# Attention and FP4 feed-forward on one core: loading the first batch's rows once, and ordering the first loads

## The chip, the cores and the metric

The kernel runs on one core of a Trainium2 chip. The metric is the device time of one execution in microseconds (us). Three runs of the kernel before gave 3693.88, 3696.45 and 3697.93; the median is 3696.45. One further execution was profiled.

The core's engines work side by side, each through its own list of instructions in order: TensorE (PE in the profile; its weight loads are PEld), VectorE (DVE), ScalarE (ACT), GpSimd (POOL) and SyncE (SP). SP here only issues transfers. Transfers of all engines share 16 DMA engines.

## The reference

The input x has 4 batches of 2048 rows of 256 numbers. One transformer block is computed:

```python
q, k, v = heads(x @ Wq.T), heads(x @ Wk.T), heads(x @ Wv.T)        # 16 heads of 16
attn = softmax(q @ k.T / 4)                                         # 2048 x 2048 for each head
x1 = layernorm(x + merge(attn @ v) @ Wo.T)
xq = fp4(x1)                                                        # blocks of 16 along a row
h = silu(xq @ fp4(w_gate).T) * (xq @ fp4(w_up).T)                   # 704 wide
out = layernorm(x1 + fp4(h) @ fp4(w_down).T)
```

All is float32; `fp4` rounds to a 4-bit grid with one scale for each block of 16 and scales back.

## The kernel before, in words

**Tiling.** A step is one batch, one block of 512 query rows (four in a batch, `NQB`) and one group of four heads: 64 steps. A step goes through 16 periods, one for each 128 keys. In a period PE computes a tile of scores for the row maxima (`maxima`, written `pm`; DVE takes the maximum, `mx`), the scores once more with the maximum subtracted (`exponentials`, `pe`; ACT takes the exponential, `e`), and the product with the values (`values`, `av`). The maxima run `LEAD` = 20 periods ahead of the exponentials. So the main loop starts with 20 lead periods, 0 to 19, in which there are only maxima and other work, and the first exponentials come in lead period 20. The program is written out in this order: PE keeps it, the other engines' lists are ordered by a scheduler.

**Other work in the periods.** Into each period goes a part (two in a lead period) of the work in `queue`: projections of x, the preparation of the weights, the feed-forward of a block whose attention is finished. `project` (L300) takes a block of 512 rows of x in `xb`, turns it on PE (`ptx`, two parts), has ACT copy it out (`xT`), and multiplies by the transposed weights (`pq` for keys and queries, `pv` for values). Which products a call makes is in `what`: `k0` and `q0` are keys and queries of heads 0 to 7, `k1` and `q1` of heads 8 to 15, `v` the values. A call makes only some of them, so the same rows are loaded and turned several times: in the first batch a block is projected for `k0`, for `v`, for `k1` and for the queries.

**Keys and queries go through device memory.** A product is split into a high and a low part (`hi`, three buffers, cast by ACT; `lo`, two buffers, by POOL from a copy of the product, `read`, two buffers). SP stores both into `kx` or `qx` (L329, four stores each). From there `load_q` (L354) and `load_k` (L363) fetch what a step needs, again on SP: four loads of 62 rows of 2 KB for the queries, four loads of 64 rows of 2 KB for each block of 512 keys. Values are stored to `vx` (L346, from two tiles `vt`) and loaded by `load_v`. Each transfer issued by SP is one instruction in SP's order; transfers take turns on eight semaphores, and one that takes a semaphore again waits until the transfer before it on the same semaphore has landed.

**Buffers for x.** `xb` (L197) has two buffers. `feed_forward` loads the same rows once more into `x1` (L588, two buffers of the same size in another pool), as the residual.

**The start.** The first two blocks of x are loaded by SP, the three weights by ACT (L207), behind which ACT fills the constant rows of `kx` (L212, four transfers of 128 KB). PE turns Wk, Wq and Wv (L214). Then lines 681 to 692 project the keys of the first batch's four blocks, and the queries of the first, with loads of x, q and k set between them. The values of the four blocks, then `k1` and `q1`, are put into `queue` and are worked off in the lead periods; the remaining queries come after them, interleaved with the preparation of the feed-forward's weights (`prepare`).

The row maxima need the keys of four periods at a time: lead periods 0, 4, 8 and 12 of the first step each begin a new block of 512 keys. In lead periods 8 to 14 the loads for the second step are asked for.

Of the kernel before, what the change touches and what calls it, by code (L numbers as in the profile page):

```python
# [31 lines left out]
F32 = mybir.dt.float32  # L32
# [6 lines left out]
P = 128  # L39
# [10 lines left out]
QT = QB // P  # L50
# [23 lines left out]
def block_kernel(  # L74
# [13 lines left out]
    B, L, D = x.shape  # L88
    FF = w_gate.shape[0]
    KC = D // P  # L90
    NQB = L // QB
# [14 lines left out]
    def psum(name):  # L106
        banks["n"] += 1
        if banks["more"] and banks["n"] % 2:
            return ps_m.tile([P, 2, 512], F32, tag="pm", name=name)[:, 0, :]
        return ps_x.tile([P, 512], F32, tag="px", name=name)  # L110
# [22 lines left out]
    def matmul(*args, **kw):  # L133
        tc.keep_in_program_order(nc.tensor.matmul(*args, **kw))  # L134

    def transpose(*args):
        tc.keep_in_program_order(nc.tensor.transpose(*args))  # L137

    def read(bank):

        t = p2.tile([P, QB // 2], F32, tag="read", name="read")[:, : bank.shape[1]]
        nc.scalar.copy(t, bank)  # L142
        return t
# [31 lines left out]
    wqT = const.tile([P, KC, D], F32, tag="wqT", name="wqT")  # L175
    wkT = const.tile([P, KC, D], F32, tag="wkT", name="wkT")
    wvT = const.tile([P, KC, D], F32, tag="wvT", name="wvT")
# [13 lines left out]
    p1 = ctx.enter_context(tc.tile_pool(name="p1", bufs=1))  # L191
    p2 = ctx.enter_context(tc.tile_pool(name="p2", bufs=2))
    xb_of = {}

    def load_x(b, tb):
        rows = slice(tb * QB, (tb + 1) * QB)
        xb_of[b, tb] = p2.tile([P, QT, D], F32, tag="xb", name="xb")  # L197
        nc.sync.dma_start(xb_of[b, tb], x[b, rows, :].rearrange("(t p) d -> p t d", p=P))

    load_x(0, 0)  # L200
    load_x(0, 1)


    loaded = {}
    for name, w in (("wk", wk), ("wq", wq), ("wv", wv)):
        loaded[name] = p2.tile([P, KC, D], F32, tag="xnh", name=name, bufs=3)
        nc.scalar.dma_start(loaded[name], w.rearrange("(c p) k -> p c k", p=P))  # L207
    ones = p2.tile([P, 2 * NC * L // P], F32, tag="a", name="ones")
    nc.gpsimd.memset(ones, 1.0)
    for i in range(2):  # L210
        for c in range(KC):
            nc.scalar.dma_start(kx[i][c][RM:R].rearrange("r h (a n) -> (r h a) n", n=2 * NC * L // P), ones)  # L212

    for name, dst in (("wk", wkT), ("wq", wqT), ("wv", wvT)):  # L214
        for kc in range(KC):
            pt = psum("ptw")
            for n in range(KC):
                transpose(pt[:, n * P : (n + 1) * P], loaded[name][:, n, kc * P : (kc + 1) * P], ident)
            if name == "wv":
                nc.vector.tensor_copy(dst[:, kc, :], pt[:, :D])  # L220
                continue

            for n in range(KC):
                nc.vector.tensor_copy(
                    dst[:, kc, n * P : (n + 1) * P].rearrange("p (d h) -> p d h", h=NC),
                    pt[:, n * P : (n + 1) * P].rearrange("p (h d) -> p d h", h=NC),
                )


    RF = FF // 8  # L230
# [69 lines left out]
    def project(b, tb, what):  # L300

        rows = slice(tb * QB, (tb + 1) * QB)
        if (b, tb) not in xb_of:
            load_x(b, tb)
        xb = xb_of.pop((b, tb))
        xT = p2.tile([P, KC, QB], F32, tag="xT", name="xT", bufs=1)
        yield 0
        for kc in range(KC):
            pt = psum("ptx")
            for t in range(QT):  # L310
                transpose(pt[:, t * P : (t + 1) * P], xb[:, t, kc * P : (kc + 1) * P], ident)
            nc.scalar.copy(xT[:, kc, :], pt)
            yield 600
        for name, c in [(w[0], int(w[1])) for w in what if w != "v"]:
            w, dst = (wkT, kx[b % 2][c][:, :, rows]) if name == "k" else (wqT, qx[(b * NQB + tb) % len(qx)][c])
            hi = p2.tile([P, QB], F32R, tag="hi", name=name + "hi", bufs=3)
            lo = p2.tile([P, QB], F32R, tag="lo", name=name + "lo", bufs=2)
            for half in range(2):
                cols = slice(half * QB // 2, (half + 1) * QB // 2)
                pq = psum("pq")[:, : QB // 2]  # L320
                for kc in range(KC):
                    matmul(pq, w[:, kc, c * P : (c + 1) * P], xT[:, kc, cols], start=(kc == 0), stop=(kc == KC - 1))
                nc.scalar.copy(hi[:, cols], pq)
                nc.gpsimd.tensor_tensor(lo[:, cols], read(pq), hi[:, cols].bitcast(F32), ALU.subtract)
                yield 900

            for i, half in enumerate((hi, lo, hi, lo) if name == "k" else (hi, hi, lo, lo)):
                d = min(DH, RM - i * DH)
                nc.sync.dma_start(  # L329
                    dst[i * DH : i * DH + d].rearrange("r h n -> (r h) n"), half[: d * NC, :].bitcast(F32)  # L330
                )
            projected.add((b, tb, name + str(c)))
        for t in range(QT if "v" in what else 0):
            v = vt[t // 2]
            pv = psum("pv")
            for kc in range(KC):
                matmul(
                    pv[:, :D], xT[:, kc, t * P : (t + 1) * P], wvT[:, kc, :], start=(kc == 0), stop=(kc == KC - 1)
                )
            src = pv[:, :D].rearrange("p (g i j d) -> p g i j d", g=NG, i=NP, j=2)  # L340
            for j in range(2):
                nc.scalar.copy(v[:, :, t % 2, :, 2 * j * DH : (2 * j + 1) * DH], src[:, :, :, j, :])
            if t % 2:
                t0 = tb * QT + t - 1
                for g in range(NG):
                    nc.sync.dma_start(vx[b % 2][g, :, t0 : t0 + 2, :], v[:, g].rearrange("p t i c -> p t (i c)"))  # L346
            if t == QT - 1:
                projected.add((b, tb, "v"))
            yield 900
# [4 lines left out]
    def load_q(s):  # L354
        b, qb, g = steps[s]
        for i in range(NP):
            c, h = divmod(g * HG + i * 2, NC)
            q = p1.tile([P, QB], F32R, tag="q", name="q", bufs=3 * NP)
            for j in range(2):
                nc.sync.dma_start(  # L360
                    q[R * j : R * j + RM, :].bitcast(F32), qx[(b * NQB + qb) % len(qx)][c][:RM, h + j, :]
                )
            q_sb[s, i] = q  # L363

    def load_k(s, kb):
        b, qb, g = steps[s]
        for i in range(NP):
            c, h = divmod(g * HG + i * 2, NC)
            k = p1.tile([P, QB], F32R, tag="k", name="k", bufs=20)
            for j in range(2):  # L370
                nc.sync.dma_start(
                    k[R * j : R * j + R, :].bitcast(F32), kx[b % 2][c][:, h + j, kb * QB : (kb + 1) * QB]
                )
            k_sb[s, i, kb] = k
# [291 lines left out]
    def projection(b, tb, what=("k0", "q0", "v", "k1", "q1")):  # L666
        return project(b, tb, what)
# [13 lines left out]
    for tb in range(NQB):  # L681
        for _ in projection(0, tb, ("k0", "q0") if tb == 0 else ("k0",)):
            pass
        if tb + 2 < NQB:
            load_x(0, tb + 2)
        if tb == 1:
            load_q(0)
        if tb > 0:
            load_k(0, tb - 1)
    load_k(0, NQB - 1)  # L690
    load_x(0, 0)
    load_x(0, 1)
    for tb in range(NQB):
        queue.append(projection(0, tb, ("v",)))
    for tb in range(NQB):
# [4 lines left out]
    for n in range(-LEAD, N + LAG):  # L700
# [10 lines left out]
        if n > 0 and kt % QT == 0:  # L711
            ahead, kb = divmod(n - QT + 2 * NKT, NKT)
            if ahead < len(steps):
                b, qb, g = steps[ahead]
# [60 lines left out]
```

## Time and profile before

| | |
|---|---|
| median of three runs | 3696.45 us |
| the profiled execution's own time | 3695.37 us |
| its span, first to last instruction | 3693.6 us |
| PE busy | 3540.7 us, 96% of the span |
| DVE busy | 2805.0 us, 76% |
| ACT busy | 2694.0 us, 73% |
| POOL busy | 1293.4 us, 35% |
| loads of x into `xb` | 27, of 512 KB each |
| loads of x into `x1` | 16, of 512 KB each |
| bytes moved by DMA | 334.18 MB, mean 90 GB/s |

How to read it: a row such as `PE L137 MATMUL ptx<-ident,xb` names the engine, the line, the operation and what is written from what. Most PE products are recorded by helper lines: L134 is every product, L137 every transpose, so they are told apart by the tiles. `SPq` is SP's issuing of a transfer, not the transfer itself. The granted PE clock is given as a share of full speed. Idle time of an engine counts only where that engine holds up the end.

### The profile page before, as it was taken

What the parts mean: (1) busy time and instruction counts of PE and PEld (TensorE: products, weight loads), DVE (VectorE), ACT (ScalarE), POOL (GpSimd) and SP (SyncE); (2) the same over time, 40 slices, a digit from 0 to 9 for tenths busy, and PEclk for the clock granted to TensorE, in tenths of its full rate; (3) what the DMA queues carried; (4) which work ended last, traced back from release to release, by engine and by line L of the source; (5) the groups of instructions that cost most, each with busy time, mean ns of one, the idle gap of its engine ahead of it and who ended that gap; (6) DMA issues with size and microseconds to landing.
All of it is one profiled execution on the core that took longest, in us unless ns stands there. A gap on an engine that the chain in (4) does not pass through costs nothing.

```text
span 3693.6 us, 57860 instructions
## 1 busy us (share of the span) xinstructions
PE 3540.7 (96%) x21396; PEld 1602.0 (43%) x21396; DVE 2805.0 (76%) x3250; ACT 2694.0 (73%) x5452; POOL 1293.4 (35%) x1542
## 2 busy tenths in 40 slices
PE   5889999999999999999999999999999999999995
PEld 4433444444444444444444444444443434444343
DVE  3777777787787877878787787778778788878834
ACT  2667777777777777777777777777777777777772
POOL 0331432424243242423424243342424325241425
PEclk8899999999999999999999999999999999999997
DMA  6643333223232332323323232322322221222100
GB/s 217 188 137 117 93 91 105 81 85 115 68 114 84 94 94 85 109 70 109 95 78 106 85 97 88 97 89 74 113 75 63 75 79 57 75 68 86 47 7 6
DMA packets 197954, 334.18 MB, mean 90 GB/s; under 512 B 26024, under 2 KB 75560, under 8 KB 197672
## 3 DMA queue, kind: packets, MB, share of 16 engines
q1 hardware_dynamic: 196280, 329.16, 29.2%
q8 instruction: 171, 2.80, 0.3%
q10 hardware_dynamic: 1392, 1.31, 0.1%
q14 instruction: 111, 0.91, 0.1%
HBM read 242.81 MB, written 86.51 MB: 89 GB/s over the span
## 4 chain that ended last, share of the span: by engine, by line
PE 82%; DVE 11%; DMA 2%; POOL 2%; SPq 1%; issue 1%; ACT 1%; ACTq 0%; POOLq 0%; DVEq 0%
PE av L134 24%; PE pe L134 18%; PE pm L134 16%; DVE mx L397 8%; PE pz L134 5%; PE pg L134 5%; PE pu L134 5%; PE pq L134 3%; PE pth L137 1%; PE pv L134 1%; PE pa L137 1%; PE py L134 1%; PE pn L137 1%; DMA k<-kx 1%; DMA xb<-in_L_attn_x_dram 1%; DVE amax L149 1%
## 5 line engine op out<-in xcount | busy, mean ns | idle before, releaser
L397 DVE TENSOR_REDUCE mx<-pm 128x2 f32<-128x1024 f32 x2048 | 2407.9, 1217 | 706.8 <-PE pm L134 702.5
L431 ACT ACTIVATE e<-pe 128x512 f32<-128x512 f32 x4096 | 2217.9, 595 | 671.2 <-PE pe L134 666.0
L134 PE MATMUL av<-e,v 128*32 128x512 f32 x8192 | 1098.3, 608 | 0.0
L134 PE MATMUL pe<-q,k 64*128 64x512 f32 x4096 | 1037.2, 456 | 4.8 <-ACT e L431 4.4
L134 PEld LDWEIGHTS pe<-q,k 64*128 64x128 f32 x4096 | 476.4, 185 | 969.0 <-ACT e L431 855.7
L134 PE MATMUL pm<-k,q 62*128 62x512 f32 x4096 | 803.8, 448 | 60.0 <-DVE mx L397 53.0
L134 PEld LDWEIGHTS pm<-k,q 62*128 62x128 f32 x4096 | 347.0, 186 | 373.2 <-issue 178.6
L134 PEld LDWEIGHTS av<-e,v 128*32 128x32 f32 x8192 | 162.2, 108 | 332.2 <-issue 314.1
L537 POOL TENSOR_TENSOR a<-a,g 128x352 f32<-128x352 f32 x124 | 116.4, 939 | 499.5 <-ACT a L536 499.5
L582 POOL TENSOR_TENSOR x<-x,read 128x128 f32<-128x128 f32 x128 | 58.9, 460 | 493.6 <-ACT read L142 493.6
L134 PE MATMUL pz<-wdT,hT 128*128 128x128 f32 (+1 forms) x1536 | 230.0, 292 | 0.0
L163 POOL TENSOR_TENSOR xn<-xn,m 128x704 f32<-128x704 f32 (+2 forms) x104 | 159.5, 1534 | 157.7 <-DVE m L162 139.0
L134 PEld LDWEIGHTS pz<-wdT,hT 128*128 128x128 f32 (+1 forms) x1536 | 191.0, 191 | 45.5 <-ACT e L431 18.2
L551 POOL TENSOR_TENSOR h<-a,u 128x352 f32<-128x352 f32 x124 | 116.2, 937 | 226.7 <-ACT u L550 224.4
L134 PE MATMUL pg<-wgT,xqT 128*128 128x352 f32 x512 | 187.4, 489 | 0.0
L513 POOL TENSOR_TENSOR x<-x,read 128x256 f32<-128x256 f32 x64 | 46.7, 730 | 400.2 <-ACT read L142 399.9
L134 PE MATMUL pu<-wuT,xqT 128*128 128x352 f32 x512 | 186.1, 486 | 0.0
L164 POOL TENSOR_TENSOR xn<-xn,m 128x704 f32<-128x704 f32 (+2 forms) x104 | 159.8, 1536 | 5.6
L165 POOL TENSOR_TENSOR xn<-xn,sc 128x704 f32<-128x704 f32 (+2 forms) x104 | 131.5, 1264 | 7.8
L538 POOL TENSOR_TENSOR a<-a,g 128x352 f32<-128x352 f32 x124 | 118.8, 958 | 9.7
L134 PEld LDWEIGHTS pg<-wgT,xqT 128*128 128x128 f32 x512 | 88.3, 191 | 58.5 <-ACT e L431 19.1
L134 PEld LDWEIGHTS pu<-wuT,xqT 128*128 128x128 f32 x512 | 88.2, 191 | 58.7 <-ACT e L431 20.0
(95 smaller groups left out, 2283.1 us busy)
## 6 DMA issues: line engine op xcount, KB each, us to landing
k<-kx SPq DMA_DIRECT2D x1024, 128.0 KB
v<-vx SPq DMA_DIRECT2D x64, 768.0 KB
q<-qx SPq DMA_DIRECT2D x256, 124.0 KB
kx<-khi SPq DMA_DIRECT2D x64, 256.0 KB
qx<-qhi SPq DMA_DIRECT2D x64, 256.0 KB
xb<-in_L_attn_x_dram SPq DMA_DIRECT2D x27, 512.0 KB
vx<-vt SPq DMA_DIRECT2D x128, 96.0 KB
x<-in_L_attn_x_dram SPq DMA_DIRECT2D x16, 512.0 KB
```

The source lines that it names most:

```text
L134: tc.keep_in_program_order(nc.tensor.matmul(*args, **kw))
L137: tc.keep_in_program_order(nc.tensor.transpose(*args))
L163: engine.tensor_tensor(xn, xn, m, ALU.add)
L164: engine.tensor_tensor(xn, xn, m, ALU.subtract)
L165: engine.tensor_tensor(xn, xn, sc.unsqueeze(2).to_broadcast([p, nb, FB]), ALU.mult)
L397: nc.vector.tensor_reduce(mx_sb[s][:, t, 2 * i : 2 * i + 2, kb], pm, AX.X, ALU.max)
L431: nc.scalar.activation(e, pe[j], AF.Exp, scale=SCALE)
L513: nc.gpsimd.tensor_add(x1[:, t, :], x1[:, t, :], read(py[:, :D]))
L537: engine.tensor_mul(a, a, g)
L538: engine.tensor_add(a, a, g)
L551: engine.tensor_mul(h[:, cols], a, u)
L582: nc.gpsimd.tensor_add(x1[:, t, cols], x1[:, t, cols], read(pz))
```

## The change

The first batch's four blocks of x are loaded once, at the start, and stay in their buffers for all their products: blocks 0 and 1 in the two `xb` buffers, blocks 2 and 3 in the two `x1` buffers, which the feed-forward doesn't need yet. `xb_of` is no longer emptied by `project`, so a later projection of the same block finds it there. The transposes of x are still made for every projection. In the first stage each block's k loads are put right behind its stores, and for block 0 the q loads right behind those; before, a block's k loads came one block later, and q after block 1. Wv is asked for last on ACT's queue among the weights, ahead of the constant fills in both built programs, and it is turned by PE after the keys of all four blocks instead of ahead of the first. In the built program the first transfers of SP are the four blocks of x and Wo, where before they were two blocks of x, Wo and two blocks for `x1`.

```diff
     def load_x(b, tb):
         rows = slice(tb * QB, (tb + 1) * QB)
-        xb_of[b, tb] = p2.tile([P, QT, D], F32, tag="xb", name="xb")
+        if b == 0 and tb >= 2:
+            xb_of[b, tb] = p1.tile([P, QT, D], F32, tag="x1", name="xb", bufs=2)
+        else:
+            xb_of[b, tb] = p2.tile([P, QT, D], F32, tag="xb", name="xb")
         nc.sync.dma_start(xb_of[b, tb], x[b, rows, :].rearrange("(t p) d -> p t d", p=P))
-    load_x(0, 0)
-    load_x(0, 1)
     loaded = {}
-    for name, w in (("wk", wk), ("wq", wq), ("wv", wv)):
+    def load_w(name, w):
         loaded[name] = p2.tile([P, KC, D], F32, tag="xnh", name=name, bufs=3)
         nc.scalar.dma_start(loaded[name], w.rearrange("(c p) k -> p c k", p=P))
+    load_x(0, 0)
+    load_w("wk", wk)
+    load_w("wq", wq)
+    for tb in range(1, NQB):
+        load_x(0, tb)
     ones = p2.tile([P, 2 * NC * L // P], F32, tag="a", name="ones")
...
-    for name, dst in (("wk", wkT), ("wq", wqT), ("wv", wvT)):
+    load_w("wv", wv)
+    def turn_w(name, dst):
         for kc in range(KC):
             pt = psum("ptw")
...
+    turn_w("wk", wkT)
+    turn_w("wq", wqT)
...
-        xb = xb_of.pop((b, tb))
+        xb = xb_of[b, tb]
...
     for tb in range(NQB):
         for _ in projection(0, tb, ("k0", "q0") if tb == 0 else ("k0",)):
             pass
-        if tb + 2 < NQB:
-            load_x(0, tb + 2)
-        if tb == 1:
+        load_k(0, tb)
+        if tb == 0:
             load_q(0)
-        if tb > 0:
-            load_k(0, tb - 1)
-    load_k(0, NQB - 1)
-    load_x(0, 0)
-    load_x(0, 1)
+    turn_w("wv", wvT)
     for tb in range(NQB):
         queue.append(projection(0, tb, ("v",)))
```

## The prediction

> **What bounds the kernel now.** I read the page's 40 slices first, then busy time by stretch, PE's waits in the first 400 us, and PE's and SP's timelines of the first 60.
>
> Busy time by stretch (columns: us, length, then busy PE, PEld, DVE, ACT, POOL with counts; granted PE clock; DMA share; GB/s):
> ```profile
> 38.00:57.40 19.40, 3.41 (x12) 2.56 (x12) 2.36 (x2) 0.59 (x1) 0.00 (x0) 0.50 0.71 225
> 57.40:62.00 4.60, 4.60 (x13) 3.02 (x12) 2.36 (x2) 1.02 (x3) 0.00 (x0) 0.50 0.50 145
> 149.00:200.00 51.00, 50.29 (x312) 21.65 (x312) 42.60 (x56) 41.48 (x87) 23.68 (x26) 1.00 0.52 166
> 315.00:3600.00 3285.00, 3241.99 (x19869) 1441.26 (x19868) 2573.23 (x2959) 2507.22 (x5032) 1160.68 (x1380) 1.00 0.28 85
> ```
> From 315 to 3600 PE is busy 98.7% of the time: there it is the bound, and the change leaves that stage's instructions alone. What it can win lies before 315. From 38 to 57.4 PE does 3.4 us of work, and is then still at half clock. What PE waits for up to 400 us (total, times, longest):
> ```profile
> PE ptx L137 <- DMA xb<-in_L_attn_x_dram: 31.4, 6, 13.8
> PE pm L134 <- DVE mx L397: 17.2, 15, 7.1
> PE pm L134 <- DMA k<-kx: 5.3, 1, 5.3
> ```
> PE's timeline (start, length; idle time before it in brackets):
> ```profile
> 29.27 1.94 PE L137 MATMUL ptx<-ident,xb 128*128 128x128 f32 x8 [5.85 <-DMA xb<-in_L_attn_x_dram]
> 40.18 1.55 PE L134 MATMUL pm<-k,q 62*128 62x512 f32 x4 [5.33 <-DMA k<-kx]
> 55.54 1.94 PE L137 MATMUL ptx<-ident,xb 128*128 128x128 f32 x8 [13.81 <-DMA xb<-in_L_attn_x_dram]
> 57.41 1.22 PE L134 MATMUL pm<-k,q 62*128 62x512 f32 x4
> 65.56 1.10 PE L137 MATMUL ptx<-ident,xb 128*128 128x128 f32 x8
> 140.18 1.09 PE L137 MATMUL ptx<-ident,xb 128*128 128x128 f32 x4 [6.01 <-DMA xb<-in_L_attn_x_dram]
> ```
> The rows for 40.18 and 57.41 are the score maxima of lead periods 0 and 1; the x reload at 55.54 stands between them. SP's queue says why:
> ```profile
> 24.61 2.36 SPq L360 DMA_DIRECT2D q<-qx  x4
> 27.02 4.77 SPq L371 DMA_DIRECT2D k<-kx  x4
> 31.89 0.54 SPq L329 DMA_DIRECT2D kx<-khi  x1
> 34.61 0.35 SPq L329 DMA_DIRECT2D kx<-klo  x1
> 37.09 0.32 SPq L329 DMA_DIRECT2D kx<-khi  x1
> 39.62 0.32 SPq L329 DMA_DIRECT2D kx<-klo  x1
> 51.21 1.08 SPq L198 DMA_DIRECT2D xb<-in_L_attn_x_dram  x2
> ```
> The x reload goes out at 51.21 because everything above stands before it. The stores at 34.61, 37.09 and 39.62 each waited for one of the q loads (SP's waits put 6.4 us on three such waits): the four q loads land about 2.5 us apart, and the k loads issued behind them only at 40.06.
>
> **What the skill says.** "DMA: Bandwidth & Descriptors", section "Why a DMA increments its semaphore by 16 and not by 1": a transfer is spread over the largest number up to 16 that divides its slowest dimension. A q load has 62 rows, so 2 engines with 31 rows of 2 KB each; a k load has 64, so 16. The trace agrees: 124 KB every 2.5 us is 50 GB/s, against over 300 for the x loads. Its section "Queues, rings and completion order" says that each engine consumes in ring order: so the k loads' shares on those two engines came after all of q. "TensorE: Matmul & The Clock Gate", "What's actually happening": an idle array drops to half clock and returns after a busy window. The trace agrees: 0.50 from 38 to 62, 1.00 from 62 to 89.
>
> **The change, step by step.** Times are those of the profiled execution.
>
> 1. *Wv last.* PE stands in order, and the first x transposes (10.38) came right behind Wv's (9.51, 1.08 us). Taken out: about 1.2 us earlier. Wv's transposes come back after the last key projection.
>
> 2. *x loaded once.* The start issues xb, xb, wo, x1, x1 now; it will issue four xb and wo: the same bytes. By slices of 1.5 us DMA moved 89 to 385 GB/s up to 12 us, 3.4 MB in all, of the 3.7 MB issued at the start (four 512 KB blocks, four weights, four 128 KB fills). So blocks 2 and 3 are there by about 13.5, needed at 19 and 22. Eleven later x loads (27 to 16) go away, about 0.5 us of SP each. The transposes stay. Key projection of block 0 and q end at 16.9 - 1.2 = 15.7; every further block takes 3.28 (16.70 to 19.98), so three end at 25.5, with Wv 26.6. The waits of 5.85 and 13.81 are gone. No buffer stops it: hi has three and the K stores of block 0 (last issued 17.50, landed 3.11 later) free one by 19.4. The lo buffers and the two read buffers make POOL wait for later stores, but block 3's casts need only block 2's lo (about 24).
>
> 3. *First k and q loads behind their stores.* The last q store is issued at 20.4 - 1.2 = 19.2 and lands as the K one did, 3.1 later: 22.3. In between SP issues the four k loads (2.4 us). The q loads follow at 22.3 to 24.7, now with almost nothing ahead of them on their two engines: landing near 25.5, 28, 30.5 and 33. The first maxima need q's first pair at 28 and the second at 33, so **the q loads are the new wait**: PE stands from 26.6 to 33 except for two matmuls. I bound this from both sides: 28.5 if q loads overlap, 38 if the backlog before them stays as it was (first landing 7 us after issue).
>
> What is queued behind on SP: block 1's K stores (from 20.57 to about 25) and everything later. Their shares on the two engines land after q, about 35.5; block 1's k loads then go out at 36 to 38 and land near 40. They are needed in lead period 4, at about 45. Blocks 2 and 3 follow each some 5 us later, needed 11 us later. Covered by 5 us; if not, PE waits one for one. The first V stores now stand behind block 2's k loads, at about 44 to 50; vt has two tiles, and PE has two product banks in hand: 0 to 4 us, I take 0.
>
> 4. *Lead period 0.* Two transposed chunks at half clock, 1.94: period 1 starts at about 35.2, where it started at 57.41. Gain **22.2**.
>
> 5. *Lead periods 1 to 20* took 115.59 - 57.41 = 58.2. x waits of 1.99, 1.31 and 2.43 go, and the half-clock window at 92.7 to 96.1 that followed one (1.2 lost). Left 51.3, against 19 x 2.69 = 51.1 by the undisturbed rhythm (65.56, 73.62, 81.64: three periods in 8.05). DVE needs 38 x 1.217 = 46.2, below that. The slow clock right after period 1 (57.4 to 62) I leave in. Further gain 6.9, **29.1** so far.
>
> 6. *The first seven periods with exponentials* took 115.59 to 148.91, 33.3. They hold the 6.01 wait and granted clocks of 0.53 and 0.84. At full speed a period is 51 us / (312 instructions / 20) = 3.27; the first two have no value products, 2.6. That gives 21.6. V's first load was issued at the start of this stage (115.39) and is used some 6 us into it; 768 KB at 300 GB/s and the 2 us or so seen around small loads fit. Of the 11.7 I take **10.4**, for short DVE waits of 0.3 to 0.6 that return.
>
> 7. *Up to 315*: PE idles 17 us in 200 to 315, most of it where DVE stands at a weight maximum (amax) whose load sits behind k loads on SP (4.4 at 204, 7.1 at 261). The SP order there is the same in both programs, so 0; bounds -5 and +5. The first x1 loads, formerly at the start, now wait for the kept blocks' last transposes; the first feed-forward begins after period 66, far later. 0.
>
> Sum 29.1 + 10.4 = 39.5. Profiled 3695.4 - 39.5 = 3655.9; the median stands 1.1 above that execution: **3657**.
>
> **Rivals.** *q comes sooner* (the four loads overlap, or PE doesn't go cold): period 0 at 28, some 5 us, and 3 to 5 of clock: about 3647. For it: no x loads in the way. Against it: three landings 2.5 apart.
>
> *A wait in place of the one removed*: block 1's k loads, or the V stores, come late behind q on those two engines, and PE stops in periods 4 to 8. For it: only 5 us of cover. 10 to 20 us given back: about 3671.
>
> *Slower*: SP stands at the second x1 load, which now waits for transposes of block 3, with the next step's k loads behind it. These are asked for 28 periods ahead of the exponentials and the maxima run 20 ahead, so 8 periods, 26 us, are covered; slower than before from a stop of 26 + 39 = 65 us: with 75, about 3706. Against it: before, an x load with a wait for PE stood in the same place, and no PE wait for k shows after 41.
>
> *No effect*: PE's later rhythm absorbs the head start, about 3696. Against it: idle is only 1.3% from 315 on.
>
> **How the numbers follow.** Likeliest 0.55 (own range 3650 to 3664), q sooner 0.2, given back 0.2, no effect 0.02, slower 0.03. The range 3643 to 3676 takes in the first two, most of the third, and the 5 us each way of step 7. A difference under 0.2% (7 us) is about what a measurement here can't tell from none: faster 0.95, same 0.02, slower 0.03.
>
> **What would show it.** PE's waits without xb up to 150; one new wait of 5 to 7 us of the first pm for q; period 1 at about 35; first pe at about 87; k loads no wait in periods 4, 8 and 12; the amax stalls still there, earlier by 39. Wrong if period 1 comes after 42, or if PE waits for k or V stores after it.

## The result, and the profile after

The changed kernel takes 3674.34 us (median of six runs, 3672.52 to 3676.19), against 3696.47 in the runs beside it: a ratio of 0.9941, 95% interval 0.9928 to 0.9953. That is 22.1 us less. The forecast was 3657, 39.5 us less: the sign and the range hold, the size is off by almost half. The profiled execution took 3676.19, its span 3674.4, so 19.2 us less than the span before.

The same stretches as before (columns: us, length, busy PE, PEld, DVE, ACT, POOL with counts; granted PE clock; DMA share; GB/s):
```profile
38.00:57.40 19.40, 17.75 (x83) 11.16 (x81) 15.59 (x15) 6.47 (x22) 1.41 (x2) 0.92 0.67 207
62.00:89.00 27.00, 20.77 (x93) 13.49 (x92) 18.15 (x18) 8.05 (x26) 2.90 (x4) 0.87 0.58 181
149.00:200.00 51.00, 45.70 (x272) 18.83 (x269) 40.10 (x49) 35.35 (x72) 21.02 (x22) 0.93 0.41 132
315.00:3600.00 3285.00, 3228.03 (x19789) 1435.47 (x19788) 2566.67 (x2965) 2495.05 (x5009) 1169.46 (x1398) 1.00 0.28 84
```
The hole from 38 to 57.4 is filled (17.75 us of PE work in place of 3.41). But 62 to 89 holds 20.8 in place of 25.0, and 149 to 200 holds 45.7 in place of 50.3: stretches that were full have got holes. The first of the two in the kernel before:
```profile
62.00:89.00 27.00, 25.01 (x123) 16.09 (x122) 23.22 (x20) 9.22 (x35) 0.00 (x0) 1.00 0.61 180
```
PE's waits up to 400 us say which (total, times, longest):
```profile
PE pm L134 <- DVE mx L409: 23.7, 21, 7.7
PE pm L134 <- DMA q<-qx: 6.2, 3, 2.7
PE ptx L137 <- ACT vt L354: 5.6, 2, 4.4
...
PE av L134 <- DMA v<-vx: 1.4, 1, 1.4
```
The 31.4 us for x are gone. New are 6.2 for q (and 1.9 that the profile puts down to a store, and that ends where the second q load is due), 5.6 for the V tiles' copies, 1.4 for V; the waits for row maxima grew from 17.2 to 23.7. PE's timeline shows the places:
```profile
28.80 0.49 PE L134 MATMUL pm<-k,q 62*128 62x512 f32 x1 [2.73 <-DMA q<-qx]
31.24 0.79 PE L134 MATMUL pm<-k,q 62*128 62x512 f32 x1 [1.94 <-DMA kx<-khi]
33.76 0.79 PE L134 MATMUL pm<-k,q 62*128 62x512 f32 x1 [1.73 <-DMA q<-qx]
36.27 0.79 PE L134 MATMUL pm<-k,q 62*128 62x512 f32 x1 [1.73 <-DMA q<-qx]
...
38.90 1.22 PE L134 MATMUL pm<-k,q 62*128 62x512 f32 x4
...
75.97 1.11 PE L137 MATMUL ptx<-ident,xb 128*128 128x128 f32 x4 [4.38 <-ACT vt L354]
...
126.63 0.79 PE L134 MATMUL pm<-k,q 62*128 62x512 f32 x2 [4.77 <-DVE mx L409]
```
The first four rows are the score maxima of lead period 0, one for each q load, 2.5 us apart.

To see where the head start is won and lost, take the time at which DVE starts the first maximum of a period, in both traces:

| period | before, us | after, us | head start | forecast |
|---|---|---|---|---|
| 1 | 58.2 | 39.7 | 18.5 | 22.2 |
| 5 | 70.6 | 50.8 | 19.8 | |
| 13 | 93.3 | 77.8 | 15.5 | |
| 20 | 116.1 | 98.0 | 18.1 | 29.1 |
| 26 | 145.9 | 118.3 | 27.6 | |
| 27 | 149.5 | 127.0 | 22.5 | 39.5 |
| 36 | 177.9 | 161.4 | 16.5 | |
| 76 | 333.4 | 315.6 | 17.8 | 39.5 |
| end of the span | 3693.6 | 3674.4 | 19.2 | 39.5 |

Two dips stand out: between periods 5 and 13, and between 26 and 36.

### The profile page after: what moved, and what is told of

It reads as the page before. It is cut to its first block, busy times and chain, and to the rows that moved or that the text cites. A ratio compares the mean times of both kernels' runs of the same rounds, so it can differ in the third digit from the quotient of the medians.

```text
span 3674.4 us, 57830 instructions
## 1 busy us (share of the span) xinstructions
PE 3535.7 (96%) x21396; PEld 1598.0 (43%) x21396; DVE 2805.1 (76%) x3250; ACT 2692.1 (73%) x5452; POOL 1292.8 (35%) x1542
## 4 chain that ended last, share of the span: by engine, by line
PE 82%; DVE 12%; POOL 3%; DMA 2%; ACT 1%; issue 1%; SPq 0%; POOLq 0%; ACTq 0%; DVEq 0%
PE av L134 24%; PE pe L134 18%; PE pm L134 15%; DVE mx L409 8%; PE pz L134 6%; PE pg L134 5%; PE pu L134 5%; PE pq L134 3%; PE pv L134 2%; PE pth L137 1%; DMA q<-qx 1%; PE pa L137 1%; PE py L134 1%; PE pn L137 1%; DVE amax L149 1%; DVE st L501 1%
## 5 line engine op out<-in xcount | busy, mean ns | idle before, releaser
L549 POOL TENSOR_TENSOR a<-a,g 128x352 f32<-128x352 f32 x124 | 116.1, 936 | 499.6 <-ACT a L548 499.6
L563 POOL TENSOR_TENSOR h<-a,u 128x352 f32<-128x352 f32 x124 | 116.1, 937 | 227.0 <-ACT u L562 224.6
L134 PEld LDWEIGHTS pg<-wgT,xqT 128*128 128x128 f32 x512 | 88.2, 191 | 58.4 <-ACT e L443 19.2
```

Of the source, the lines that this page charges most:

```text
L549: engine.tensor_mul(a, a, g)
L563: engine.tensor_mul(h[:, cols], a, u)
```

## Experiments

Two theories of the missing half were set against each other. **A:** a q load has 62 rows and runs on two DMA engines only, 2.5 us each, and whatever has a share on these two engines waits behind it; the first maxima, the V stores and the weights' loads all pay. **B:** these transfers are late because of SP's order and of what is queued ahead of them, whatever the spread of q. A second question was which part of the change brings the 22 us.

### Spreading q for the first step alone, and for all steps

```diff
             for j in range(2):
-                nc.sync.dma_start(
-                    q[R * j : R * j + RM, :].bitcast(F32), qx[(b * NQB + qb) % len(qx)][c][:RM, h + j, :]
-                )
+                for r0, r1 in ((0, 32), (32, RM)) if s == 0 else ((0, RM),):
+                    nc.sync.dma_start(
+                        q[R * j + r0 : R * j + r1, :].bitcast(F32),
+                        qx[(b * NQB + qb) % len(qx)][c][r0:r1, h + j, :],
+                    )
```
The second kernel has the split in every step (without the `if`).

> The changed kernel; only the first step's four q loads of 62 rows are issued as 32 and 30 rows each, so that each spreads over 16 and 15 engines in place of 2. Theory A (a q load's 62 rows run on two engines, 2.5 us each, and this is what the first maxima wait for): the four q loads are down by about 30 in place of 36.3, lead period 1 starts at 32 to 34 in place of 38.9; of the 5 to 7 us a part is given back at the later waits (V tiles, weight maxima), which this edit leaves: end 2 to 6 us below the changed kernel's 3674. Theory B (they land late because of the stores queued ahead and the way of a small load, whatever its spread): landings as before or later, because SP issues four more, period 1 at 38.9 to 40, end 3674 to 3677.

> The changed kernel with every q load of every step issued as 32 and 30 rows. Theory A: besides the first wait, the V tiles' waits in lead periods 7 to 13 (1.2 and 4.4 us before transposes of x) and the weight maximum's wait of 4.8 us at 127 shrink, because V stores and weight loads no longer have their shares behind q's on two engines: lead over the kernel before at period 40 about 27 to 35 us in place of 16.5, end 3655 to 3665. Theory B (these waits are SP's order: each transfer is issued late, whatever its spread): the waits stay, SP issues four more per step, end 3670 to 3677.

The first took 3666.18 us (ratio to before 0.9918, 95% interval 0.9903 to 0.9933), the second 3651.11 (0.9877, 0.9862 to 0.9891): both faster than theory A had it. PE's timeline with the first step's q spread:
```profile
26.90 0.47 PE L134 MATMUL pm<-k,q 62*128 62x512 f32 x1 [0.43 <-DMA q<-qx]
...
44.44 2.08 PE L134 MATMUL pv<-wvT,xT 128*128 128x256 f32 x4 [3.71 <-ACT vt L354]
...
118.05 0.79 PE L134 MATMUL pm<-k,q 62*128 62x512 f32 x2 [4.71 <-DVE mx L411]
```
All of q is down by 27 in place of 36.3, and the first maximum of period 1 starts at 28.9 in place of 39.7. That is 10.9 us, more than the 5 to 7 expected; 8.2 are left at the end. Of the 10.9, 1.9 are not the spread of the load: SP issues the first q load at 21.6 in place of 23.5, 0.7 because its list runs that much earlier from the first store on; the rest isn't explained. (One possible reason: the split's first piece holds the rows of the high parts alone, which are stored first.) The wait of 4.7 for the weights stays, as it should: only step 0 was changed. PE's waits up to 400 us with q spread in all steps:
```profile
PE pm L134 <- DVE mx L411: 10.8, 19, 1.6
...
PE av L134 <- DMA v<-vx: 4.2, 1, 4.2
PE pv L134 <- ACT vt L354: 2.2, 1, 2.2
```
The waits for row maxima fall from 23.7 to 10.8, and none is longer than 1.6 (7.7 in the changed kernel): the stalls behind the weights' loads are gone. So are the waits for V tiles in lead periods 9 and 12. But one of 2.2 us in period 5 has come up, before any q load of the second step is issued, and V's first load is now late by 4.2. At period 40 this kernel is 25.0 us ahead of the one before, where theory A had 27 to 35.

### The same number of transfers, spread less

The control: 31 and 31 rows in place of 32 and 30, once for step 0 and once for all steps.
```diff
-                for r0, r1 in ((0, 32), (32, RM)):
+                for r0, r1 in ((0, 31), (31, RM)):
```


> The changed kernel; the first step's q loads issued as 31 and 31 rows: as many transfers as with 32 and 30, but 31 is divided only by 1, so by theory A every one of the eight runs on one and the same engine, about 2.5 us each: the last lands 20 us after the first starts, near 43 to 46, and period 1 starts near 46 to 49 in place of 38.9. If it is the smaller transfers and not their spread that helped, period 1 starts near 29 as with 32 and 30 rows.

> The changed kernel with every q load of every step issued as 31 and 31 rows: the same number of transfers as with 32 and 30 in every step, but each on one engine. Theory A (the spread counts): the waits for V tiles and for the weights' loads grow past those of the changed kernel, end above 3690. Rival (with twice as many q transfers SP's list is ordered otherwise, and that is what shortened the later waits): end within 6 us of the 3651 of 32 and 30 rows, but for the first wait's 18 us, so 3651 to 3672.

One execution of each: 3686.14 and 3714.43 us. PE's timeline with 31 and 31 rows in step 0:
```profile
34.91 0.76 PE L134 MATMUL pm<-k,q 62*128 62x512 f32 x1 [4.59 <-DMA q<-qx]
39.95 0.76 PE L134 MATMUL pm<-k,q 62*128 62x512 f32 x1 [4.28 <-DMA q<-qx]
45.04 0.76 PE L134 MATMUL pm<-k,q 62*128 62x512 f32 x1 [4.33 <-DMA q<-qx]
```
The pairs land 5.1 us apart, twice the 2.5 of 62 rows; with 32 and 30 rows it was 0.9, which is SP's pace of issuing them. DVE's first maximum of period 1 starts at 48.5 in place of 39.7, as theory A said. PE's waits up to 400 us with 31 and 31 rows in all steps:
```profile
PE pm L134 <- DVE mx L411: 40.4, 18, 13.4
PE pm L134 <- DMA q<-qx: 12.9, 3, 4.3
PE pq L134 <- ACT vt L354: 11.4, 1, 11.4
...
PE av L134 <- DMA v<-vx: 3.6, 1, 3.6
```
This kernel and the one with 32 and 30 rows issue the same 2315 transfers on SP in the same order. The waits for row maxima are 40.4 against 10.8, for the V copies 11.4 against 2.2; the two kernels are 24.1 us apart in lead period 18 and 61.5 in period 76. So these stalls of the row maxima and the 11.4 us for the V copies come from the spread of q, and theory B falls for them. V's first load is late in both (3.6 and 4.2). Whether theory B holds for the lead periods is for the next experiments.

The Trainium skill's rule ("DMA: Bandwidth & Descriptors", "Why a DMA increments its semaphore by 16 and not by 1": the largest number up to 16 that divides the slowest dimension) gives 2, 1, and 16 with 15 engines for 62, 31, and 32 with 30 rows. The measured steps of 2.5, 5.1 and 0.9 us go with it. So does the busy share of the 16 DMA engines in stretches in which, and for 5 us before which, SP has issued nothing but q loads; first the changed kernel, then all q as 31 and 31 rows:
```profile
107.00:109.00 2.00, 2.00 (x12) 1.16 (x10) 0.00 (x0) 1.30 (x3) 0.00 (x0) 1.00 0.13 50
26.00:30.00 4.00, 0.76 (x1) 0.28 (x1) 0.00 (x0) 0.00 (x0) 0.00 (x0) 0.76 0.06 25
```
A share of 0.13 is two engines of 16, and 0.06 is one, at half the rate.

### The parts of the change

x loaded once, and nothing else: the loads of all four blocks at the start, `xb_of[b, tb]` in place of `pop`, and
```diff
-        if tb + 2 < NQB:
-            load_x(0, tb + 2)
         if tb == 1:
             load_q(0)
         if tb > 0:
             load_k(0, tb - 1)
     load_k(0, NQB - 1)
-    load_x(0, 0)
-    load_x(0, 1)
```
The order of the q and k loads, and nothing else:
```diff
-        if tb == 1:
-            load_q(0)
-        if tb > 0:
-            load_k(0, tb - 1)
-    load_k(0, NQB - 1)
+        load_k(0, tb)
+        if tb == 0:
+            load_q(0)
```


> The kernel before with one part of the change alone: x of the first batch loaded once, at the start; q and k loads and Wv stay where they were. Theory A: the q loads stand behind block 1's stores as before and land by about 38, period 0 at about 38 to 40 and period 1 at about 42 in place of 57.4: 12 to 16 us of head start, end about 3676 to 3682. Rival (the order of the first q and k loads brings most of it): head start under 8, end 3688 to 3696.

> The kernel before with another part alone: each block's k loads right behind its stores, and q behind block 0's; x is loaded again for each projection and Wv turned first, as before. Theory A: the x reloads stay behind k loads and stores on SP and are waited for by PE; blocks 2 and 3 still wait for x; the period 1 reload comes perhaps 5 us earlier: end 3688 to 3696. Rival (the order brings most): end 3676 to 3682.

x once alone: 3674.99 us (0.9940, 0.9924 to 0.9957), the same as the whole change. The order alone: 3704.76, slower (1.0021, 1.0012 to 1.0029), which neither side had expected. x once alone, PE's timeline:
```profile
38.53 1.55 PE L134 MATMUL pm<-k,q 62*128 62x512 f32 x4 [12.34 <-DMA k<-kx]
...
72.79 1.35 PE L134 MATMUL pv<-wvT,xT 128*128 128x256 f32 x4 [2.38 <-ACT vt L345]
```
The first maxima wait for k behind q and start at 38.5; period 1 starts 3 us later than with the whole change (42.7 against 39.7), but less is lost to V, and by period 20 it is 2.1 us ahead. The order alone:
```profile
41.34 1.94 PE L137 MATMUL ptx<-ident,xb 128*128 128x128 f32 x8 [18.20 <-DMA xb<-in_L_attn_x_dram]
...
88.31 1.94 PE L137 MATMUL ptx<-ident,xb 128*128 128x128 f32 x8 [11.33 <-DMA xb<-in_L_attn_x_dram]
```
Here the q loads are issued at 23.97 and block 3's x at 30.56, behind them and block 1's stores; it lands at 41. Before, it was issued at 23.87, ahead of q, and PE waited 5.9 us for it. From 36 to 40 two engines alone are at work while PE waits for this x, and SP has issued nothing since a store at 31.80:
```profile
36.00:38.00 2.00, 0.00 (x0) 0.00 (x0) 0.00 (x0) 0.00 (x0) 0.00 (x0) 0.50 0.13 50
```
The waits for x sum to 52.1 us in place of 31.4.

### q spread in the kernel before, and with x loaded once

> The kernel before with every q load issued as 32 and 30 rows; x reloads, order and Wv as before. Theory A (two-engine q loads cost the start in both kernels and delay the weights' loads up to 300): the k wait at 40.18 goes, the x reload leaves SP earlier, the stalls of 4.4 and 7.1 us at 204 and 261 shrink: 10 to 22 us faster than before, end 3675 to 3686; the change is then worth more beside spread q loads than without. Rival (only the changed kernel suffers, since it alone puts q where PE waits for it): under 5 us, end 3691 to 3697.

> x loaded once, q and k loads and Wv as in the kernel before, every q load as 32 and 30 rows. It tells what the change's new order is worth once q is spread. Theory A: with q spread, k and q of block 0 are down near 31 in the old order against 26 in the new one, so period 1 is 3 to 6 us later than with the order changed (29.7): end 3652 to 3657 against 3651. Rival (the order doesn't matter even then, since later waits level it out): 3649 to 3652.

The edits are those above, joined. The kernel before with q spread takes 3678.10 us (0.9947, 0.9932 to 0.9962), with x loaded once as well 3647.62 (0.9865, 0.9850 to 0.9879). The four medians:

| | q loads of 62 rows | q loads of 32 and 30 rows |
|---|---|---|
| the kernel before | 3696.5 | 3678.1 |
| x once, old order | 3675.0 | 3647.6 |
| the whole change | 3674.3 | 3651.1 |

x once is worth 21.5 us beside narrow q loads and 30.5 beside spread ones: theory A's expectation. With narrow q loads (62 rows) the new order changes nothing that can be told; with spread ones the whole change is 3.5 us slower than the old order, where we had expected 3 to 6 faster. Period 1 is indeed 6.9 us earlier with it (29.7 against 36.6), but by period 12 the old order has caught up. By period 23 it is 3.6 us ahead; of these, 2.3 are that V's load is waited for 1.9 us there and 4.2 with the new order.

The lengths of the stretches between DVE's first maxima, from the one profiled execution of each, tell which part acts where (us):

| | periods 1 to 20 | 20 to 27 | 27 to 36 | 36 to 76 |
|---|---|---|---|---|
| the kernel before | 57.8 | 33.4 | 28.5 | 155.5 |
| the same, q spread | 58.5 | 32.0 | 33.5 | 140.1 |
| x once, old order | 53.1 | 28.9 | 31.2 | 158.1 |
| the same, q spread | 50.3 | 26.0 | 34.9 | 139.7 |
| the whole change | 58.3 | 29.0 | 34.4 | 154.2 |
| the same, q spread | 57.7 | 30.6 | 35.0 | 139.9 |

Spreading q brings 14 to 18 us between periods 36 and 76, in all three kernels. In periods 1 to 20 it is the order that counts: the whole change takes 5.2 us longer there than x once in the old order, and 7.4 longer with q spread, while spreading q in the whole change brings only 0.6. With the old order SP issues the k loads of all four blocks before the first V store; with the new one the first V stores come between the k loads of blocks 2 and 3. PE waits 5.9 us for the V tiles' copies in this stretch with the whole change, 2.4 with x once; with q spread 2.2 and nothing, and the granted clock is 0.89 and 0.99. So for the lead periods theory B has the larger share.

### V's first load earlier, and Wv last

```diff
-        if n == 0:
+        if n == -4:
             load_v(0)
```


> The changed kernel with every q load as 32 and 30 rows and, besides, the first step's value load asked for four periods earlier. The wait of 4.2 us before the first value product goes: end about 3647 if the lead is kept, 3651 if the weight maxima's waits at 120 to 150 take it back.

> x loaded once, q loads as 32 and 30 rows, the old order of the first q and k loads, Wv first as before, and the first value load asked for four periods earlier. The wait of 1.9 us before the first value product goes: 3643 to 3646 where it stood at 3647.6 without the early load; if the order of the q and k loads costs nothing and only V's lateness did, it equals the 3645.7 of the same with the changed order.

> The same with Wv turned last. PE has the first x transposes 1.0 to 1.2 us earlier; but it waits for block 0's k and q afterwards (4.4 us where q is spread and the old order kept), and those stand behind block 1's stores, which also come 1 us earlier: 0.5 to 1.5 us faster than with Wv first if the start is one chain, nothing if the wait is for something else.

With the changed order 3645.69 us (0.9862, 0.9846 to 0.9879): 5.4 less than without the early load, the wait for V is gone. With the old order 3646.28: 1.3 less. The two are equal within their runs, so at the end V's late load accounts for what the new order had cost. Both now take 23 us from period 20 to 27. Wv turned last, in the old order, gives 3644.88 (3642.70 to 3645.40, against 3645.36 to 3647.95): 1.4 less, as large as expected but hardly clear of the spread. Its lead periods 1 to 20 take 51.7 us against 56.4 for the new order, which turns Wv last too: so Wv is not what makes the new order longer there. This is the fastest version of the study (ratio 0.9856, 0.9842 to 0.9871), some 29 us below the changed kernel.

## Why the prediction was right, and where its size went wrong

The mechanism of the gain was right: the end is set before 315 us, the x reloads behind SP's queue held PE up, and PE keeps its head start afterwards (17.8 at period 76, 19.2 at the end). The account of what follows the start was not. Of the signs that I had named, period 1 came at 38.9 for 35, the first exponentials at 98.5 for 87, and "wrong if PE waits for k or V stores after it" came true: PE waits 5.9 us for the V tiles' copies. The median lies in the range by under 2 us, near the 3671 of a rival to which I gave 0.2; that is as much the width of the range as the reasoning. The profiled 19.2 against 39.5 is 20.3 us, step by step:

**Steps 1 and 2 hold.** The first x transposes start at 8.77 in place of 10.38 (1.2 forecast, 1.6 measured), no projection waits for x, and the last ends at 25.6 (25.5 forecast).

**Steps 3 and 4: right wait, 3.7 us too small.** PE waits for four q loads 2.5 us apart. SP's timeline after:
```profile
19.65 2.68 SPq L383 DMA_DIRECT2D k<-kx  x4
23.51 1.33 SPq L372 DMA_DIRECT2D q<-qx  x4
...
38.74 2.37 SPq L383 DMA_DIRECT2D k<-kx  x4
...
44.05 2.37 SPq L383 DMA_DIRECT2D k<-kx  x4
46.47 0.58 SPq L341 DMA_DIRECT2D kx<-klo  x1
47.15 2.37 SPq L358 DMA_DIRECT2D vx<-vt  x4
50.36 2.37 SPq L383 DMA_DIRECT2D k<-kx  x4
```
The q loads are issued at 23.5 in place of 22.3, because the last q store took 4.68 to land and not 3.1, and the first is down 5.3 after its issue in place of 3.2. What held it the 2 us longer isn't shown. Period 1 on PE: 38.9 in place of 35.2.

**Step 5: the 6.9 us did not come; this is where "0 to 4 us, I take 0" failed.** Lead periods 1 to 20 took 58.3 us in place of 51.3. The V stores are issued at 47, 53 and later, between k loads, as foreseen. ACT waits for a V tile, PE for ACT: 1.23 and 4.38 us in periods 9 and 12, with a granted clock of 0.51 from 75 to 82 behind it. In these periods the second step's q loads stand among the V stores, and SP itself waits 5.0 us, three times, for a q load to land before it issues a V store; with q spread in all steps the waits there are gone. But others take their place, and the stretch is only 0.6 us shorter. With the old order of the k and q loads it is 53.1 us, with q spread besides 50.3, a little less than the forecast. So what I put at nothing is the cost of V stores set between k loads. That the order costs this is shown by the pairs of runs; that it acts through the V stores is read from PE's waits. My rival of a wait in place of the one removed, with the V stores late behind q, comes near to it, in later periods than 4 to 8 and with q as the smaller part.

**Step 6: up to period 26 it came, then it was taken back.** The head start rose from 18.1 at period 20 to 27.6 at 26, 9.5 of the 10.4. At 27 it is 22.5. What took it back is the first weight block, on DVE before:
```profile
140.89 0.68 DVE L149 TENSOR_REDUCE amax<-wl 88x32 f32<-88x512 f32 x1 [6.39 <-DMA wl<-in_L_ffn_w_gate_dram]
```
and after, with the transfers around it on SP:
```profile
124.76 0.68 DVE L149 TENSOR_REDUCE amax<-wl 88x32 f32<-88x512 f32 x1 [5.21 <-DMA wl<-in_L_ffn_w_gate_dram]
```
```profile
111.93 5.12 SPq L383 DMA_DIRECT2D k<-kx  x4
117.28 0.35 SPq L263 DMA_DIRECT2D wl<-in_L_ffn_w_gate_dram  x1
117.86 8.06 SPq L383 DMA_DIRECT2D k<-kx  x8
```
Before, DVE's wait ended at 140.89, and PE stood waiting for x until 140.18 anyway: the weight wait was free. I counted that x wait of 6.01 as a gain and did not ask what else it covered. After, DVE's wait stops the row maxima and PE with them, 4.77 us. The weight is issued at 117.28 and used 7.5 us later. That narrow q loads make it late is shown by the pair with equal SP order, not by this line: as 31 and 31 rows it is used 10.2 us after its issue and DVE waits 9.2, as 32 and 30 rows 5.7 and DVE doesn't wait. With q spread and V's load early the stretch from 20 to 27 takes 23.1 us, close to the 22.9 that I had for it.

**Step 7: "the SP order there is the same, so 0" came out as 4.7 lost, near my bound of 5.** But for the x loads the order is the same, and so is the sum of DVE's waits for weights from period 20 on (22.8 us before, 23.4 after); in the changed kernel less of it is covered. Six microseconds go between periods 27 and 36, some 3 of them in smaller waits of this kind (0.9, 0.9, 0.6 and 0.4 on PE), with a granted clock of 0.79 from 126 to 134 and from 157 to 165. The rest I did not take apart. Spreading q doesn't bring them back: this stretch is then as long (35.0). Why it is shorter in the kernel before (28.5) isn't shown. 1.3 come back by period 76 and 1.4 by the end.

The terms: 3.7 (steps 3 and 4), 7.3 (step 5: 6.9 and the 0.4 lost), 6.0 (step 6: 10.4 less the 4.4 left at period 27), 4.7 (step 7), less 1.4 after period 76: 20.3.

The rivals: "q comes sooner" did not happen by itself; made to happen by spreading the first step's loads, it gave 8.2 us, near the 10 that I had for it. "Slower" through SP standing at the second x1 load left no trace. The change's order of q and k loads, which I treated as a gain, is worth nothing here: x loaded once alone gives the same time. It brings period 1 3.0 us forward and loses 5.2 by period 20.

## What to carry to other kernels

Before a removed wait is booked as a gain, look at what the other engines wait for under it: a wait of DVE that was free beneath PE's becomes the next bound. Count a transfer by the engines that it runs on, not by its bytes, and carry that on to every transfer that has a share on the same engines. When loads are moved forward in a queue, ask what now stands behind them: here the stores of V. And a reordering is best tried beside each of the other parts: here loading x once brought everything, and the order gave nothing with narrow q, cost 3.5 us with q spread, and cost 8 us alone.

## What the runs showed of the hardware

Loads of 124 KB in 62 rows of 2 KB land 2.5 us apart, at 50 GB/s, with a busy share of two DMA engines of 16; as 31 and 31 rows a pair takes 5.1 us, at 25 GB/s, with the share of one; as 32 and 30 rows a pair takes 0.9 us, which is SP's pace of issuing. SP needs 3.72 us to issue the eight pieces against 1.33 for four. A transfer issued behind such loads lands late: block 3's 512 KB of x took 10.8 us from issue to use with the order alone, with two engines at work in the last part of it, where x loads that PE waited for took 4.3 to 6.4 in the kernel before. Spreading the q loads of the kernel before, with no other edit, is worth 19 us of 3697.
